# Adapter products of a unit's two halves from partitions 0 and 64, and the second gate's logits by experts in four quadrants

## The chip, the cores and the metric

The kernel runs on one core of one Trainium2 chip. The metric is the device time of one execution in microseconds; the time of a kernel is the median of its runs. Engines are named as in the profile: PE is TensorE, DVE VectorE, ACT ScalarE, POOL GpSimd, SP the queue that issues most DMAs.

## What is computed

The input x has 8 batches of 256 tokens of 128 features. Two layers follow each other, each added to its input, each with a conditioning step and a feed-forward over 8 experts of width 512. All is float32.

```python
# layer 0: masked pooling over the batch's tokens, then all 8 experts on every token, weighted by kept gate logits
pooled = softmax(mask(tanh(x @ W1 + b1) @ v)) @ x / count
logits = pooled @ gate_weight.T            # kept where >= the value at rank 4*128*6 of all, else 0
x = x + sum_e gates[..., e] * (gelu_tanh(pooled @ w1[e].T + b1[e]) @ w2[e].T + b2[e])
# layer 1: an adapter chosen by the batch's language, layer norm, then the 2 best of 8 experts per token
h = relu(x @ W1[lang] + b1[lang])          # 128 -> 32
a = layernorm(x + h @ W2[lang] + b2[lang]) * gamma[lang] + beta[lang]      # 32 -> 128
xn = layernorm(a) * gamma + beta
w = top-2 of softmax(xn @ gate_w), made to sum to 1
x = x + a + sum_e w_e * (gelu(xn @ w1[e] + b1[e]) @ w2[e] + b2[e])
```

## The kernel before

The 2048 tokens are 16 tiles of 128. They are handled in five units: units 0, 1 and 2 are four tiles each (two batches), units 3 and 4 are two tiles each (one batch). GT is 4, P is 128, D is 128, A is 32, E is 8.

**Layer 0.** The first hp_first starts at 36.1 us, after the pooling of the first batches. From there `layer` loops over units and, in each, over the 8 experts: four products hp_first (L801, up to 128x512), each with its GELU on ScalarE (L803), and, one expert behind, four accumulated products yp_first (L781). VectorE multiplies each yp_first by its gates, which SP loads spread over the partitions (gbc_first, L761), and adds it up in acc_first (L769, L771).

**What runs behind.** A queue of generators, `behind`, is worked off between those products: `pump()` takes one step of the first generator, up to its next `yield`, at each call. After a unit's last expert, `adapt(u)` is put into this queue, so units 0 to 3 are adapted behind the products of later units, and unit 4 behind layer 1. A scheduler then orders the instructions of every engine by its own estimate of when they can run; each engine's order is fixed when the kernel is built.

**`adapt(u)`** goes through these steps:
- x2T, the unit's x by features, is acc_first plus xT (L578). fp (L459) turns acc_first to tokens, and x2 (L582) is x by tokens.
- adp (L588): for each of the unit's batches one product of lw1 (128x32, the batch's language) with that batch's 256 columns of x2T. All outputs lie on partitions 0 to 31 of one PSUM bank, side by side. ha (L590) is the ReLU with the bias, one VectorE instruction per batch; its 33rd row is set to one by POOL (L586), which carries the bias of the next product.
- dp (L595): for each tile one product of 33 rows of ha with lw2 (33x128), all into one bank. xr (L598) adds x2 to it in one instruction.
- Two layer norms (`normed`: statistics on VectorE, the power rstd_l and rstd_f on POOL, L475), and the rows zr for the experts.
- znp (L624) turns the rows to features, znT (L629) scales them.
- l1p (L635): for each tile the logits of the second gate, with the tile's znT as stationary operand (128x128) and the 8 columns of the gate's weights streamed. lg (L638) copies them, `top_one` twice picks two experts per token.
- kp (L666, L667) counts, by products with ones and a triangle, how many earlier tokens went to each expert; from that pos (L686) is each token's row, and POOL scatters the rows to xs in DRAM, one indirect DMA a tile and choice (L688), eight in a unit of four tiles.
- For units 2, 3 and 4, lists of the expert tiles that are then full are made (`listed`).

**Layer 1.** 36 expert tiles of 128 rows. `fetch(k)` has SP load the rows xt (L831) and the first weights wt (L839) of the expert named in the list: tiles 0 to 16 come from unit 2's list, 17 to 20 from unit 3's, and from 21 on unit 4's. A load waits until the scatters that can fill it have landed. `turn` transposes (xtp, L846), `hidden` makes four products hps (L857) and the GELU hs (L859), `output` four products yps (L866), bias (L870), weight (L871) and an indirect DMA to ys (L872) from POOL. At the end ys is loaded again (yg, L890), added to the residual (L899, L900) and stored (L904).

**Buffers.** PSUM is cut into four banks "big" (psb: hp_first, adp, dp, znp, hps), two "y" (psy: yp_first, yps) and two "sm" (pss: fp, l1p, kp, xtp). ha has two buffers.

**Loads of the adapters.** Near the start SP reads each batch's language number and loads lw1, lw2 and the language's gamma and beta (lgb), three DMAs for each of 8 batches (L164).

Of the kernel before, what the change touches and what calls it, by code (L numbers as in the profile page):

```python
# [10 lines left out]
F32 = mybir.dt.float32  # L11
I32 = mybir.dt.int32
AF = mybir.ActivationFunctionType
ALU = mybir.AluOpType
AX = mybir.AxisListType
SYNC = mybir.DependencyInfo(mybir.DependencyClass.Sync, mybir.DependencyReason.DATA)
SP, PE, DVE = mybir.EngineType.SP, mybir.EngineType.PE, mybir.EngineType.DVE
# [4 lines left out]
B, S, D = 8, 256, 128  # L22
P = 128
NT = B * S // P
NG = 4
GT = NT // NG
GN = GT * P

UNITS = [(0, 0, 4), (1, 0, 4), (2, 0, 4), (3, 0, 2), (3, 2, 2)]
NU = len(UNITS)  # L30
SLOTS = {2: 17, 3: 21, 4: 39}
E, HC = 8, 4
A = 32
NL = 10
KTH = 4 * 128 * 6 - 1
NEG = -1.0e30
# [21 lines left out]
C_W1 = 0  # L58
C_G0 = C_W1 + A
C_G1 = C_G0 + E  # L60
# [5 lines left out]
C_LB = C_LG + 1  # L66
NCOL = C_LB + 1
XW = D + E + 1


@with_exitstack
def tile_adaln_ffn_d2(ctx: ExitStack, tc: tile.TileContext, x, ptype, lang, cols, b1v,
                      w10, w20, w11d, w21d, lw1, lw2, lgb, out):
    nc = tc.nc
# [3 lines left out]
    const = ctx.enter_context(tc.tile_pool(name="const", bufs=1))  # L78
    first = ctx.enter_context(tc.tile_pool(name="first", bufs=E))
    keep = ctx.enter_context(tc.tile_pool(name="keep", bufs=NG))  # L80
    work = ctx.enter_context(tc.tile_pool(name="work", bufs=2))
    small = ctx.enter_context(tc.tile_pool(name="small", bufs=4))
    dram = ctx.enter_context(tc.tile_pool(name="dram", bufs=1, space=DRAM))
    psb = ctx.enter_context(tc.tile_pool(name="psb", bufs=4, space=PSUM))
    psy = ctx.enter_context(tc.tile_pool(name="psy", bufs=2, space=PSUM))
    pss = ctx.enter_context(tc.tile_pool(name="pss", bufs=2, space=PSUM))
# [4 lines left out]
    for g in range(NG):  # L91

        xg.append(keep.tile([P, GT, XW], F32, tag="xg", name=f"xg{g}"))
    ptb = const.tile([P, B], I32, name="ptb")
    lgi = const.tile([P, B], I32, name="lgi")
    col = const.tile([P, NCOL], F32, name="col")
    bva = const.tile([A, 2], F32, name="bva")
    ident = const.tile([P, P], F32, name="ident")
# [10 lines left out]
    for e in range(E):  # L109
        t = first.tile([P, HC * P], F32, tag="w1", name=f"w10_{e}")  # L110
        nc.sync.dma_start(out=t, in_=w10[e])
        w10s.append(t)
        t = first.tile([P, HC, D], F32, tag="w2", name=f"w20_{e}")
# [4 lines left out]
    for g in range(NG):  # L118
        nc.gpsimd.memset(xg[g][:, :, XW - 1:], 1.0)
    ones = const.tile([P, P], F32, name="ones")  # L120
# [31 lines left out]
    nc.vector.tensor_scalar(out8[:, 2:3], out8[:, 2:3], -1.0, NEG, ALU.mult, ALU.add)  # L152


    lws, las, lgs = [], [], []
    for b in range(B):
        at = nc.values_load(lgi[0:1, b:b + 1], engines=(SP,), min_val=0, max_val=NL - 1,
                            skip_runtime_bounds_check_because="a language's number")
        for lst, name, src, rows, width in (
                (lws, "lw1", lw1[bass.ds(at * P, P), :], P, A),  # L160
                (las, "lw2", lw2[bass.ds(at * (A + 1), A + 1), :], A + 1, D + 1),
                (lgs, "lgb", lgb[bass.ds(at, 1), :].rearrange("o w -> (o w)").partition_broadcast(P), P, 2 * D)):
            t = const.tile([rows, width], F32, name=f"{name}_{b}")
            nc.sync.dma_start(out=t, in_=src)  # L164
            lst.append(t)

# [13 lines left out]
    front = work.tile([P, HC, GN], F32, tag="hT", name="front").rearrange("p c n -> p (c n)")  # L180
    at = front[:, :GN].rearrange("p (g t a) -> p g t a", g=NG, a=A)
    fwd, bwd, top = (front[:, GN + i * S:GN + (i + 1) * S] for i in range(3))
    fwd, bwd, rows = fwd[:B, :], bwd[:B, :], top[:B, :]
# [17 lines left out]
    def products(g):  # L201

        space = (psy, "y") if g < 2 else (psb, "big")
        xa = space[0].tile([P, GT, A + E], F32, tag=space[1], name=f"xa{g}")
        for t in range(GT):
# [18 lines left out]
    for g in range(NG):  # L224
# [8 lines left out]
        if not g:  # L233
            nc.tensor.matmul(bvp.rearrange("p c a -> p (c a)"), lhsT=ones[:A, :],
                             rhs=diag.rearrange("k c a -> k (c a)"), start=True, stop=True)
# [9 lines left out]
    for b in range(B):  # L245
        kinds.append(nc.values_load(kind[0:1, b:b + 1], engines=(DVE,), min_val=0, max_val=2,
                                    skip_runtime_bounds_check_because="2 - 2 e0 - e1, of flags"))
# [14 lines left out]
    for g in range(NG):  # L262
        tp = psb.tile([P, 2, S], F32, tag="big", name=f"top{g}")
        for i in range(2):
            nc.tensor.matmul(tp[:, i, :], lhsT=ident[:, 2 * g + i:2 * g + i + 1].to_broadcast([P, P]), rhs=top,
                             start=True, stop=True)
# [15 lines left out]
    def pool(b, space):  # L282
        m, g, i = masks[b], b // 2, b % 2
        pp = space[0].tile([P, 2, XW], F32, tag=space[1], name=f"poolp{b}")
        for jt in range(2):
# [104 lines left out]
    while known < half + 1:  # L390
        n = min(known, half + 1 - known)
# [126 lines left out]
    for e in range(E):  # L518
        nc.sync.dma_start(out=w21[:, e, :], in_=w21d[e].rearrange("p c d -> p (c d)"))
    nc.sync.dma_start(out=b2all.rearrange("p e d -> p (e d)"),  # L520
                      in_=b2d.rearrange("e d -> (e d)").partition_broadcast(P))
    rows = xs.rearrange("(p m t) c -> p m (t c)", p=P, t=GT)
# [11 lines left out]
    def tiles_of(counts, edges, name, f=None):  # L534

        c2 = small.tile([P, E, NT], F32, tag="c2", name=f"c2_{name}", bufs=1)
        nc.vector.tensor_tensor(c2, counts.unsqueeze(2).to_broadcast([P, E, NT]),
                                edges.unsqueeze(1).to_broadcast([P, E, NT]), ALU.is_ge)
        if f is None:
            f = small.tile([P, E], F32, tag="f", name=f"nf_{name}", bufs=2)  # L540
        nc.vector.tensor_reduce(f, c2, AX.X, ALU.add)
        return f
# [30 lines left out]
    def adapt(u, acc):  # L573
        g, o, nt = UNITS[u]
        n, t0 = nt * P, g * GT + o
        batches = range(t0 // 2, (t0 + nt) // 2)
        x2T = work.tile([P, GN], F32, tag="x2T", name=f"x2T{u}")[:, :n]
# [3 lines left out]
        x2 = work.tile([P, GT, D], F32, tag="x2", name=f"x2_{u}")[:, :nt, :]  # L581
        nc.vector.tensor_tensor(x2, fp, xg[g][:, o:o + nt, :D], ALU.add)  # L582
        yield
        hp = psb.tile([A, 2, S], F32, tag="big", name=f"adp{u}")
        ha = work.tile([A + 1, 2, S], F32, tag="ha", name=f"ha{u}")
        nc.gpsimd.memset(ha[A:A + 1, :, :], 1.0)  # L586
        for i, b in enumerate(batches):
            nc.tensor.matmul(hp[:, i, :], lhsT=lws[b], rhs=x2T[:, i * S:(i + 1) * S], start=True, stop=True)  # L588
        for i, b in enumerate(batches):
            nc.vector.tensor_scalar(ha[:A, i, :], hp[:, i, :], las[b][:A, D:D + 1], 0.0, ALU.add, ALU.max)  # L590
        yield
        yield
        dp = psb.tile([P, GT, D], F32, tag="big", name=f"dp{u}")[:, :nt, :]
        for t in range(nt):
            nc.tensor.matmul(dp[:, t, :], lhsT=ha[:, t // 2, (t % 2) * P:(t % 2 + 1) * P],  # L595
                             rhs=las[batches[t // 2]][:, :D], start=True, stop=True)
        z = work.tile([P, GT, D], F32, tag="xr", name=f"xr{u}")[:, :nt, :]
        nc.vector.tensor_tensor(z, dp, x2, ALU.add)  # L598
        yield
        yield from normed(z, z, f"l{u}")  # L600
        yield
# [23 lines left out]
        if nt == GT:  # L625
            zt = keep.tile([P, GN], F32, tag="poolT", name=f"znT{u}")
        else:
            zt = work.tile([P, n], F32, tag="znT", name=f"znT{u}", bufs=1)
# [1 line left out]
                                col[:, C_LB:C_LB + 1], ALU.mult, ALU.add)  # L630
        yield
        yield
        lp = pss.tile([P, GT, E], F32, tag="sm", name=f"l1p{u}")[:, :nt, :]
        for t in range(nt):
            nc.tensor.matmul(lp[:, t, :], lhsT=zt[:, t * P:(t + 1) * P], rhs=col[:, C_G1:C_G1 + E],  # L635
                             start=True, stop=True)
        lg = small.tile([P, GT, E], F32, tag="ex", name=f"lg{u}")[:, :nt, :]
        nc.vector.tensor_copy(lg, lp)  # L638
        oh1, l1 = top_one(lg, f"p{u}")
# [31 lines left out]
        at = small.tile([P, GT, E], F32, tag="at", name=f"at_{u}")[:, :nt, :]  # L671
# [9 lines left out]
        for s, oh in enumerate((oh1, oh2)):  # L681
# [5 lines left out]
            for t in range(nt):  # L687
                move = nc.gpsimd.indirect_dma_start(  # L688
                    out=xs, out_offset=bass.IndirectOffsetOnAxis(ap=pos[:, t:t + 1], axis=0),
                    in_=zr[s][:, t, :], in_offset=None)  # L690
# [8 lines left out]
        if u in SLOTS:  # L699

            k0, k1 = SLOTS.get(u - 1, 0), SLOTS[u]
            f = tiles_of(counts, begun if u == NU - 1 else full, str(u))
# [218 lines left out]
    def early():  # L921
        for k in range(LEAD + PRIMED):
            ahead(k)
        for _ in range(PRIMED):
            flipped.append(turn(*fetched.popleft()))

    behind.append(run("poolings", poolings()))
    behind.append(run("threshold", threshold()))
    layer("first", AF.Gelu_apprx_tanh, poolT, w10s, w20s, C_B10, C_B20, gates0, "pool", adapt,
          early)  # L930

# [16 lines left out]
    while behind:  # L948
# [3 lines left out]
                          skip_runtime_bounds_check_because="a count of tiles")  # L952
# [62 lines left out]
```

## Time and profile before

| | us |
|---|---|
| median of 3 runs | 379.78 |
| lowest and highest | 378.04, 383.52 |
| the profiled execution | 373.48 |
| its span, first to last instruction | 371.8 |

| engine | busy, us | share | instructions |
|---|---|---|---|
| PE | 349.5 | 94% | 1596 |
| PEld | 237.9 | 64% | 1596 |
| DVE | 198.9 | 53% | 835 |
| ACT | 166.6 | 45% | 387 |
| POOL | 95.5 | 26% | 141 |

PE is the matrix multiply and PEld the load of its stationary operand. A line of the timeline gives start, duration, engine, source line, operation, output<-inputs, shapes and a count, and in brackets how long the engine stood idle before it and what ended that. A line of a waits view gives engine, output and line that waited, what released it, and total us, times and longest. A line of the groups gives engine, operation and shape with the count, then busy us and mean ns of one, then idle before it. Durations of products overlap with those of their neighbours; the time from one group's start to the next group's start is what the group took from the engine.

### The profile page before, as it was taken

Reading aid. Unit: us, or ns where it says so; the run is one execution under the profiler, and the core shown is the slowest. Engines: PE = TensorE matmul, PEld = TensorE weight load, DVE = VectorE, ACT = ScalarE, POOL = GpSimd, SP = SyncE. Lnnn points to the kernel's source line nnn. Section 1 sums busy time; section 2 is a strip of 40 time slices with the busy share of each in tenths; the row PEclk is TensorE's granted clock in tenths of the full one; section 3 lists DMA queues with packets and bytes.
Section 4 is the critical chain, followed back from the end, with each engine's and each line's share of the span. In section 5 each row is a group of like instructions: output and inputs, shape, how many; then the busy total and the mean of one; then the engine's idle time right before and its main releaser. Section 6 shows DMA issues by size and latency. Waiting matters only on the chain. (4 is left out here: it accounts for less than half of the span.)

```text
span 371.8 us, 5944 instructions
## 1 busy us (share of the span) xinstructions
PE 349.5 (94%) x1596; PEld 237.9 (64%) x1596; DVE 198.9 (53%) x835; ACT 166.6 (45%) x387; POOL 95.5 (26%) x141
## 2 busy tenths in 40 slices
PE   6999999999999999999999999999999989989950
PEld 5979545444444444544544468887887989979940
DVE  3358465554314567556461146578658668433353
ACT  2116733454453324522335233643563675857650
POOL 8100000000000003055126001207304656744550
PEclk9999999999999999999999999999999999999995
DMA  6934899200523321111013000112474355576556
GB/s 187 389 89 135 301 382 379 88 0 2 160 71 81 91 56 31 56 60 54 31 36 89 16 28 21 45 36 80 129 178 145 113 168 154 164 192 203 151 172 198
DMA packets 34466, 46.12 MB, mean 124 GB/s; under 512 B 5444, under 2 KB 17622, under 8 KB 34432
## 3 DMA queue, kind: packets, MB, share of 16 engines
q1 hardware_dynamic: 29888, 39.98, 35.3%
q0 software_dynamic: 2304, 4.37, 3.4%
q10 hardware_dynamic: 2240, 1.38, 1.2%
q8 instruction: 14, 0.23, 0.3%
q14 instruction: 20, 0.16, 0.1%
HBM read 31.57 MB, written 14.39 MB: 124 GB/s over the span
## 5 line engine op out<-in xcount | busy, mean ns | idle before, releaser
L803 ACT ACTIVATE hT_first<-hp_first,col 128x512 f32<-128x512 f32 (+1 forms) x160 | 93.5, 601 | 101.2 <-PE hp_first L801 101.0
L801 PE MATMUL hp_first<-poolT,w 128*128 128x512 f32 (+1 forms) x320 | 120.6, 512 | 0.0
L781 PE MATMUL yp_first<-hT_first,w 128*128 128x512 f32 (+1 forms) x320 | 120.5, 511 | 0.0
L781 PEld LDWEIGHTS yp_first<-hT_first,w 128*128 128x128 f32 x320 | 58.9, 190 | 42.5 <-issue 38.3
L801 PEld LDWEIGHTS hp_first<-poolT,w 128*128 128x128 f32 x320 | 59.0, 190 | 42.2 <-issue 36.8
L688 POOL DMA_INDIRECT xs<-zr,pos x32 | 32.2, 1008 | 65.3 <-DVE pos L686 27.9
L859 ACT ACTIVATE hs<-hps,b 128x128 f32<-128x128 f32 x144 | 40.5, 373 | 9.5 <-PE hps L857 9.5
L872 POOL DMA_INDIRECT ys<-yt,xt x36 | 35.5, 987 | 32.9 <-ACT hs L859 21.1
L769 DVE SCALAR_TENSOR_TENSOR part_first<-yp_first,col,gbc_first 128x512 f32<-128x512 f32 (+1 forms) x28 | 17.2, 615 | 40.5 <-PE yp_first L781 40.3
L866 PE MATMUL yps<-w,hs 128*128 x288 | 38.0, 276 | 0.5 <-ACT hs L859 0.5
L857 PE MATMUL hps<-xc,wt 128*128 128x128 f32 x288 | 38.2, 276 | 0.0
L857 PEld LDWEIGHTS hps<-xc,wt 128*128 128x128 f32 x288 | 35.1, 192 | 0.6 <-issue 0.4
L866 PEld LDWEIGHTS yps<-w,hs 128*128 128x128 f32 x288 | 35.0, 192 | 0.6 <-ACT hs L859 0.6
L871 ACT ACTIVATE yt<-yt,xt 128x128 f32<-128x128 f32 x36 | 14.8, 413 | 18.3 <-ACT hs L859 7.3
L410 POOL DMA_DIRECT2D gd_L<-gT_L x1 | 0.7, 653 | 81.2 <-DVE gT_L L408 81.2
L771 DVE TENSOR_TENSOR acc_first<-acc_first,part_first 128x512 f32<-128x512 f32 (+1 forms) x35 | 20.1, 580 | 0.6
L586 POOL MEMSET ha<- 1x512 f32 x5 | 2.6, 516 | 67.6 <-PE dp L595 67.4
L850 DVE COPY b<-col 128x4 f32 x36 | 7.0, 196 | 20.8 <-ACT hs L859 18.1
L789 ACT ACTIVATE y_first<-yp_first,col 128x512 f32<-128x512 f32 x8 | 5.5, 687 | 24.2 <-PE yp_first L781 24.2
L848 DVE TENSOR_SCALAR xc<-xtp,col 128x128 f32<-128x128 f32 x36 | 14.4, 401 | 1.9 <-PE xtp L846 1.9
L870 DVE TENSOR_TENSOR yt<-yps,b2all 128x128 f32<-128x128 f32 x36 | 10.4, 290 | 9.1 <-PE yps L866 7.9
L424 DVE TENSOR_SCALAR_CACHE_REDUCE fl<-logit,tr 128x128 f32<-128x128 f32 x46 | 13.5, 343 | 0.6
(213 smaller groups left out, 327.9 us busy)
## 6 DMA issues: line engine op xcount, KB each, us to landing
wt<-in_w_dram SPq DMA_DIRECT2D x36, 256.0 KB
xs<-empty SPq DMA_DIRECT2D x1, 8580.0 KB
w<-in_w_dram SPq DMA_DIRECT2D x24, 256.0 KB
gbc_first<-gd_L SPq DMA_DIRECT2D x24, 256.0 KB
xt<-xs SPq DMA_DIRECT2D x36, 65.0 KB
gbc_first<-gd_L SPq DMA_DIRECT2D x16, 128.0 KB
yg<-ys SPq DMA_DIRECT2D x5, 256.0 KB
lgb<-in_lgb_dram SPq DMA_DIRECT2D x8, 128.0 KB
```

The costliest lines, as they stand in the source:

```text
L688: move = nc.gpsimd.indirect_dma_start(out=xs, out_offset=bass.IndirectOffsetOnAxis(ap=pos[:, t:t + 1], axis=0), in_=zr[s][:, t, :], in_off ...
L769: nc.vector.scalar_tensor_tensor(part, y, bias, gbc, ALU.add, ALU.mult)
L771: nc.vector.tensor_tensor(accs[u], accs[u], part, ALU.add)
L781: nc.tensor.matmul(yp, lhsT=w2s[e][:, c, :], rhs=hT[:, c, :], start=(c == 0), stop=(c == HC - 1))
L801: nc.tensor.matmul(hp, lhsT=w1s[e][:, c * P:(c + 1) * P], rhs=sources[g][:, o * P:o * P + n], start=True, stop=True)
L803: nc.scalar.activation(hT[:, c, :], hp, act, bias=col[:, cb1 + e * HC + c:cb1 + e * HC + c + 1])
L848: nc.vector.tensor_scalar(xc, tp, col[:, C_LG:C_LG + 1], col[:, C_LB:C_LB + 1], ALU.mult, ALU.add)
L857: nc.tensor.matmul(hp[:, c, :], lhsT=wt[:, c * P:(c + 1) * P], rhs=xc, start=True, stop=True)
L859: nc.scalar.activation(hT[:, c, :], hp[:, c, :], AF.Gelu, bias=b1[:, c:c + 1])
L866: nc.tensor.matmul(yp, lhsT=hT[:, c, :], rhs=w21[:, bass.ds(ek, 1), c * D:(c + 1) * D], start=(c == 0), stop=(c == HC - 1))
L871: nc.scalar.activation(yt, yt, AF.Copy, scale=xt[:, D + 1:D + 2])
L872: move = nc.gpsimd.indirect_dma_start(out=ys, out_offset=bass.IndirectOffsetOnAxis(ap=xt.bitcast(I32)[:, D:D + 1], axis=0), in_=yt, in_off ...
```

## The change

There are three edits, and the loads that go with them.

1. `halves(u)` gives the batches of a unit's two halves: two batches, or the same batch twice. For each half, adp's product writes its own partitions: 0 to 31 for the first, 64 to 95 for the second, in the same columns of the bank. In a unit of two tiles each half is 128 columns of the one batch, so there are two products of 128 columns where there was one of 256. ha has the two halves on partitions 0 to 32 and 64 to 96, with a row of ones at 32 and at 96.
2. dp's products of the first half read partitions 0 to 32, those of the second 64 to 96. They alternate, and each half has a PSUM tile of its own, two "big" banks where there was one. The sum xr is one instruction per half.
3. In units of four tiles the logits are made the other way round: 32 columns of `col` from the gate's 8 on are the stationary operand, and a tile's 128 columns of znT are streamed; tile t's result goes to partitions 32t to 32t + 31 of one bank (l1q). Of each 32 rows the first 8 are the logits. VectorE copies the bank (l1s), two `yield`s follow, one transpose on PE turns it to tokens (l1p), and lg reads 8 of every 32 columns. Units of two tiles are as before.
4. lw2 is loaded into one tile per unit, once for each half, so the two small units load theirs twice: ten loads of lw2 where there were eight. The language numbers are read ahead of the loads in the program.

```diff
+LANE = 64
...
+def halves(u):
+
+    g, o, nt = UNITS[u]
+    b = (g * GT + o) // 2
+    return (b, b + 1) if nt == GT else (b, b)
...
+    for u, (g, o, nt) in enumerate(UNITS):
+        la = const.tile([LANE + A + 1, D + 1], F32, name=f"lw2_{u}")
+        las.append(la)
+        for i, b in enumerate(halves(u)):
...
+            nc.sync.dma_start(out=la[i * LANE:i * LANE + A + 1, :], in_=lw2[bass.ds(langs[b] * (A + 1), A + 1), :])
...
-        hp = psb.tile([A, 2, S], F32, tag="big", name=f"adp{u}")
-        ha = work.tile([A + 1, 2, S], F32, tag="ha", name=f"ha{u}")
-        nc.gpsimd.memset(ha[A:A + 1, :, :], 1.0)
-        for i, b in enumerate(batches):
-            nc.tensor.matmul(hp[:, i, :], lhsT=lws[b], rhs=x2T[:, i * S:(i + 1) * S], start=True, stop=True)
-        for i, b in enumerate(batches):
-            nc.vector.tensor_scalar(ha[:A, i, :], hp[:, i, :], las[b][:A, D:D + 1], 0.0, ALU.add, ALU.max)
+        m, lanes = n // 2, [slice(0, A), slice(LANE, LANE + A)]
+        hp = psb.tile([LANE + A, S], F32, tag="big", name=f"adp{u}")[:, :m]
+        ha = work.tile([LANE + A + 1, S], F32, tag="ha", name=f"ha{u}")[:, :m]
+        for lane in lanes:
+            nc.gpsimd.memset(ha[lane.stop:lane.stop + 1, :], 1.0)
+        for i, b in enumerate(halves(u)):
+            nc.tensor.matmul(hp[lanes[i], :], lhsT=lws[b], rhs=x2T[:, i * m:(i + 1) * m], start=True, stop=True)
+        for lane in lanes:
+            nc.vector.tensor_scalar(ha[lane, :], hp[lane, :], las[u][lane, D:D + 1], 0.0, ALU.add, ALU.max)
...
-        dp = psb.tile([P, GT, D], F32, tag="big", name=f"dp{u}")[:, :nt, :]
-        for t in range(nt):
-            nc.tensor.matmul(dp[:, t, :], lhsT=ha[:, t // 2, (t % 2) * P:(t % 2 + 1) * P],
-                             rhs=las[batches[t // 2]][:, :D], start=True, stop=True)
+        dps = [psb.tile([P, 2, D], F32, tag="big", name=f"dp{u}_{i}") for i in range(2)]
+        for t in range(nt // 2):
+            for i, lane in enumerate(lanes):
+                rows = slice(lane.start, lane.stop + 1)
+                nc.tensor.matmul(dps[i][:, t, :], lhsT=ha[rows, t * P:(t + 1) * P], rhs=las[u][rows, :D],
+                                 start=True, stop=True)
...
-        nc.vector.tensor_tensor(z, dp, x2, ALU.add)
+        for i in range(2):
+            part = slice(i * nt // 2, (i + 1) * nt // 2)
+            nc.vector.tensor_tensor(z[:, part, :], dps[i][:, :nt // 2, :], x2[:, part, :], ALU.add)
...
+        if nt == GT:
+
+            lq = pss.tile([P, P], F32, tag="sm", name=f"l1q{u}")
+            for t in range(nt):
+                nc.tensor.matmul(lq[t * A:(t + 1) * A, :], lhsT=col[:, C_G1:C_G1 + A], rhs=zt[:, t * P:(t + 1) * P],
+                                 start=True, stop=True)
+            ls = work.tile([P, P], F32, tag="gT", name=f"l1s{u}")
+            nc.vector.tensor_copy(ls, lq)
+            yield
+            yield
+            lp = pss.tile([P, GT, A], F32, tag="sm", name=f"l1p{u}")
+            nc.tensor.transpose(lp.rearrange("p t c -> p (t c)"), ls, ident)
+            lp = lp[:, :, :E]
+        else:
...
```

In the order that the scheduler makes of the changed kernel, the transpose of the logits stands two hp_first products (units 0 and 1) or four (unit 2) behind l1q. Unit 4's kp stands three yps and three hps products further back on PE than before. On POOL its rstd_l stands one output scatter further ahead, and one more output scatter stands ahead of its four scatters to xs instead of between them.

More of the change, by code (lines that the diff above doesn't have):

```diff
@@ L155, in tile_adaln_ffn_d2 @@
     lws, las, lgs = [], [], []
[L156 to L165, printed above, removed]
+    langs = [nc.values_load(lgi[0:1, b:b + 1], engines=(SP,), min_val=0, max_val=NL - 1,
+                            skip_runtime_bounds_check_because="a language's number") for b in range(B)]
+    for u, (g, o, nt) in enumerate(UNITS):
+        la = const.tile([LANE + A + 1, D + 1], F32, name=f"lw2_{u}")
+        las.append(la)
+        for i, b in enumerate(halves(u)):
+            if nt == GT or not i:
+                t = const.tile([P, A], F32, name=f"lw1_{b}")
+                nc.sync.dma_start(out=t, in_=lw1[bass.ds(langs[b] * P, P), :])
+                lws.append(t)
+            nc.sync.dma_start(out=la[i * LANE:i * LANE + A + 1, :], in_=lw2[bass.ds(langs[b] * (A + 1), A + 1), :])
+            if nt == GT or not i:
+                t = const.tile([P, 2 * D], F32, name=f"lgb_{b}")
+                nc.sync.dma_start(out=t, in_=lgb[bass.ds(langs[b], 1), :].rearrange("o w -> (o w)").partition_broadcast(P))
+                lgs.append(t)
     logit = const.tile([P, E, NT], F32, name="logit")
@@ L632, in adapt @@
         yield
[L633 to L636, printed above, removed]
+        if nt == GT:
[11 more added lines that the diff above has]
+        else:
+            lp = pss.tile([P, GT, E], F32, tag="sm", name=f"l1p{u}")[:, :nt, :]
+            for t in range(nt):
+                nc.tensor.matmul(lp[:, t, :], lhsT=zt[:, t * P:(t + 1) * P], rhs=col[:, C_G1:C_G1 + E],
+                                 start=True, stop=True)
         lg = small.tile([P, GT, E], F32, tag="ex", name=f"lg{u}")[:, :nt, :]
```

## The prediction

> **What bounds the kernel now.** I read the page first, then the waits of TensorE, then the timeline of TensorE around the first unit's adapter, then the groups of the lines that change, and last the timelines where the last unit's rows reach the expert tiles.
>
> ```profile
> PE 349.5 (94%) x1596; PEld 237.9 (64%) x1596; DVE 198.9 (53%) x835; ACT 166.6 (45%) x387; POOL 95.5 (26%) x141
> ...
> PE   6999999999999999999999999999999989989950
> ```
>
> TensorE is busy 8 or 9 tenths in every slice from the second to the thirty-eighth. A busy row can hide waits, so the second view is its list of waits:
>
> ```profile
> PE idle L193 <- POOL ident masks.py:199: 2.6, 1, 2.6
> PE xtp L846 <- DMA xt<-xs: 1.7, 1, 1.7
> PE kp L666 <- DVE sofar L660: 1.2, 1, 1.2
> PE znp L624 <- DVE zr L478: 0.8, 1, 0.8
> ```
>
> After the start it waits some 4 us in all. TensorE's own work, in its order, is the bound, so time taken from its queue comes off the end, except where one of these waits takes it back. The third view gives what the touched lines cost, read from start to next start (the durations overlap and are too long for that):
>
> ```profile
> 132.73 1.05 PE L588 MATMUL adp<-x2T,lw 128*32 128x256 f32 x4
> 133.71 1.98 PE L781 MATMUL yp_first<-hT_first,w 128*128 128x512 f32 x4
> 135.62 1.16 PE L595 MATMUL dp<-lw,ha 33*128 33x128 f32 x8
> 136.71 1.98 PE L781 MATMUL yp_first<-hT_first,w 128*128 128x512 f32 x4
> 138.53 3.60 PE L801 MATMUL hp_first<-poolT,w 128*128 128x512 f32 x8
> 141.96 3.60 PE L781 MATMUL yp_first<-hT_first,w 128*128 128x512 f32 x8
> ...
> 153.56 0.95 PE L635 MATMUL l1p<-col,znT 128*128 128x8 f32 x8
> 154.37 2.82 PE L801 MATMUL hp_first<-poolT,w 128*128 128x512 f32 x6
> ```
>
> adp takes 133.71 - 132.73 = 0.98 us, dp 1.09, l1p 0.81. Units 1 and 2 give 0.98, 1.08 to 1.09 and 0.81 again; the units of two tiles give 0.55 for adp and 0.64 for dp. All the touched work is 3 x 2.88 + 2 x 1.19 = 11.0 us, 2.9% of the run: no speed-up of it can bring more than that.
>
> ```profile
> L595 PE MATMUL dp<-lw,ha 33*128 33x128 f32 x32 | 4.9, 288 | 0.0
> L588 PE MATMUL adp<-x2T,lw 128*32 128x256 f32 x16 | 4.4, 386 | 0.0
> L635 PEld LDWEIGHTS l1p<-col,znT 128*128 128x128 f32 x32 | 4.3, 191 | 1.1 <-DVE znT L629 0.5 <-issue 0.5
> ```
>
> The counts matter: 8 written adp products stand as 16 records and 16 dp products as 32. A written f32 product is two load-and-multiply pairs on the same part of the array, one after the other.
>
> **The skill.** The Trainium skill's "TensorEngine Tiling (Array Packing)", Key Properties, says that different tiles of the array load and multiply in parallel, and that changing the tiling mode drains TensorE. Its "TensorE: Matmul & The Clock Gate", Part 3 ("What overlaps and what doesn't"), says that multiplies start and end in program order, a second tile's some 4 ns after the first's, and gives 3.07x for four row tiles and 2.38x for three column tiles, at 512 columns. No run of before uses two tiles, so overlap isn't shown here. The drain fits: hp_first gives 3.43 / 8 = 0.429 us for 512 columns, so 0.214 for 256 and 0.107 for 128; adp's four passes then leave 0.98 - 0.86 = 0.12 us over and dp's eight 1.09 - 0.86 = 0.23. The tiling page's Gotcha 1 says that row tiles must write different PSUM banks; that is why dp becomes two tiles.
>
> **The change, part by part.** *adp.* The two halves go to columns 0 and 64. In program order the passes are a0 a1 b0 b1; a1 must follow a0 in its tile, b0 may run beside a1, b1 follows: three slots for four. A four-tile unit saves 0.21 us. A two-tile unit replaces two passes of 256 (0.43) by four of 128 in three slots (0.32): 0.11. Bounds: nothing (no overlap), or two slots (0.43 and 0.21 saved).
>
> *dp.* Lanes alternate, eight passes of 128: a0, a1 with b0, b1 with the next a0 and so on, five slots: 0.32 saved, and 0.11 in a two-tile unit. The weight loads are 128 wide and fill these slots too, so this needs loads of the two row halves to run side by side. Bounds: nothing saved, or 0.43.
>
> *Logits.* Today 0.81 us: eight loads of 128 columns, 0.10 each, for 8 streamed columns. New: four products with 32 weight columns streaming 128, eight passes. By the same rule five slots, 0.53, plus a switch of mode as adp's, 0.12, plus one transpose at 0.11 (znp: four in 151.84 - 151.40 = 0.44): 0.77, a saving of 0.05. Bounds: no overlap, 0.86 + 0.23 = 1.09, which loses 0.27; four quadrants together, two slots, 0.44, which saves 0.37. This part can lose; it is near even.
>
> Sum over TensorE: 3 x (0.21 + 0.32 + 0.05) + 2 x (0.11 + 0.11) = 1.74 + 0.44 = 2.2 us, 0.2 of it in unit 4.
>
> *New waits.* The transpose waits for VectorE's copy of 128x128 from PSUM (the row of gT_L has 0.29 us), in units 0 to 2. Behind the waiting transpose in TensorE's order stand all the expert products, for which ScalarE waits. The order that the scheduler gave puts two products of 512 columns (1.7 us) or four of 256 ahead of it, cover for one VectorE instruction in progress (at most 0.81 in its rows) and the copy. Without that cover it would be 1 us a unit; with it I take 0.1 each, 0.3 in all, bounds 0 to 2. The gate's chain of these units gets later by two pump steps; unit 2's rows are first loaded at 262.33 and first used at 278.76, so 16 us hide the 1 to 2 us.
>
> *VectorE.* Per four-tile unit one more copy (0.29) and the sum over dp in two of 256 columns (2 x 0.42 for 0.69); VectorE is at 53% and gets 0.45 us more: nothing. PSUM: dp holds two of the four "big" banks. The next product that needs either comes behind at least four other passes or after yps and hps; dp's sum starts within 1.2 us of it, so nothing, and up to 1 us if VectorE runs late.
>
> *SP and POOL.* Ten loads of lw2 where there were eight: two more on SP at some 0.45 us each (two lw loads take 0.87) between 15.5 and 32 us, in front of w21 and the fill of xs. The next thing in that queue that can be late is gbc_first at 94.57, which waits for gd_L anyway. The memset of ha becomes two rows of half the length; the queue behind it is held by the same dp as before. Nothing.
>
> *Unit 4's chain.* This is where the saving can be given back. Its rows are finished only during the expert tiles:
>
> ```profile
> 315.15 0.95 POOL L688 DMA_INDIRECT xs<-zr,pos  x1 [0.30 <-issue]
> ```
>
> ```profile
> 325.16 1.07 SPq L831 DMA_DIRECT2D xt<-xs  x1
> ...
> 327.73 0.30 PE L846 MATMUL xtp<-ident,xt 128*128 128x128 f32 x1 [1.71 <-DMA xt<-xs]
> ```
>
> From the end of the last acc_first (283.16) to this transpose run 44.6 us, a chain through VectorE, POOL and DMAs, and TensorE waits 1.71 us for it. What TensorE saves inside that stretch, 0.2 us, only lengthens the wait; what it saves before 283 moves the start of the chain and counts in full. What lengthens the chain counts in full too. ha becomes two instructions of 128 columns (0.33 each by the slope, for 0.47) and the sum two (0.29 each for 0.42): +0.35 us. Against it, POOL's rstd_l of unit 4 comes ahead of an output scatter that it stands behind today (its input is done at 290.71, it starts at 292.01): up to -1.3. Both end at kp, whose place in TensorE's order is now three yps and three hps products further back (six times 0.22 us, 1.3), while today it holds TensorE for 1.21 us: kp runs 0.1 us later than before, with its inputs ready. After kp, POOL sends one more output scatter ahead of unit 4's four instead of between them, so the last of the four keeps its place. I take 0.2, bounds -0.5 to 2.
>
> **Together.** -2.0 (before 283) + 0.3 + 0.2 = -1.5 us. The profiled execution took 373.48 (span 371.8 and 1.68 around it), so I expect 372.0 there. The median of the runs shown, 379.78, is 6.3 higher; nothing in the change touches that, so 378.3. A measurement of this kernel can tell about 2% from no change, 7.6 us; the forecast lies within.
>
> **The rivals.**
> *All passes overlap* (the upper bounds: 3 x 1.23 + 2 x 0.43 = 4.5, 4.1 of it before 283; with a chain unchanged and 0.1 for the waits): -4.0, 375.8. For it speak the skill's two factors; against it that a product's two passes share one tile and end in order.
> *Nothing overlaps*: adp and dp as before, logits 3 x 0.27 = +0.8, waits 0.3, chain 0.2: +1.3, 381.1. For it: l1p at 0.10 us for 8 columns shows that loads alone can be the bound, and dp's are as wide.
> *Slower by unit 4's chain*: its last scatter leaves POOL at 315.15, 32.0 us after the last acc_first. Each microsecond more goes to the end. From 33.7 us (the 1.7 that is saved) the kernel is slower than before; with two tiles' time (2 x 1.89 us, the step from one xtp to the next) it is 379.78 - 1.7 + 3.8 = 381.9. For it: the chain already makes TensorE wait, the scheduler moved kp back and an output scatter ahead. Against: POOL's last scatter keeps its place.
>
> **How the numbers follow.** Forecast 0.53, full overlap 0.22, no overlap 0.13, late chain 0.12. The runs shown spread over 378.04 to 383.52, 1.4%, so a case 4 us from the old median can come out past 2%. Faster by over 2%: half of full overlap and a little of the forecast, 0.17. Slower by over 2%: half of the late chain, and 0.04 of the others, 0.10. Within 2%: 0.73. The range goes from full overlap less the spread, 373.8, to the late chain with a little more, 383.0.
>
> **What would show it.** adp's block from 0.98 to about 0.77 us from start to next start, dp's from 1.09 to 0.77, l1q and the transpose together 0.7 to 0.8; records of one lane that start beside the other's. The last acc_first some 1.7 us earlier, and a wait of xtp for xt of 1.7 to 3 us. I am wrong if the blocks keep their length, if a transpose waits over 0.5 us for l1s, if hp_first waits for dp's banks, or if a wait over 4 us stands at xtp.

## The result, and the profile after

Median 377.50 us (372.88 to 384.24, 22 runs) against 379.94 us for the kernel before in the same measurement (376.03 to 385.04, 22 runs): ratio 0.9941, 95% interval 0.9914 to 0.9968. That is 2.2 us less by the ratio and 2.4 between the medians; 1.5 were forecast. The profiled execution took 377.19 us, span 375.4.

An execution starts in one of two ways, with the first hp_first at 29.0 to 31.4 us or at 36.1 to 36.4 us in the profiles here, and the kernel before shows both. Where two traces are compared below, times are therefore counted from that first hp_first. This execution ends 346.35 us after it, and the profiled one of before 335.66 us after its own, although the medians go the other way; the experiments on the third chip bear on that.

The page, first the busy times, then TensorE's busy tenths and its granted clock in 40 slices:

```profile
PE 344.7 (92%) x1603; PEld 230.1 (61%) x1603; DVE 200.3 (53%) x845; ACT 167.1 (45%) x387; POOL 96.1 (26%) x146
...
PE   6899999999999999999999999989979996999940
...
PEclk9999999999999999999999999999998998999995
```

TensorE is busy 4.8 us less than before, and still the engine without gaps until about the 27th slice. Then come holes that the profile of before did not have, and its list of waits shows two sorts of them:

```profile
PE xtp L882 <- DVE xc L884: 2.6, 2, 1.9
PE xtp L882 <- issue: 1.9, 2, 1.1
PE kp L702 <- DVE sofar L696: 1.8, 4, 0.8
PE yps L902 <- issue: 1.7, 2, 1.4
PE hp_first L837 <- issue: 1.1, 2, 0.6
```

The third line is a dependence: kp waited once before, in unit 4; now it waits four times. The lines that end in "issue" are time in which TensorE waits for nothing that the profile shows. The experiments separate the two.

TensorE's timeline around unit 0's adapter and second gate; blocks are read from start to next start, as for before:

```profile
125.67 0.62 PE L605 MATMUL adp<-x2T,lw 128*32 128x256 f32 x4
126.23 1.98 PE L817 MATMUL yp_first<-hT_first,w 128*128 128x512 f32 x4
128.14 0.71 PE L615 MATMUL dp<-lw,ha 33*128 33x128 f32 x8
128.79 1.98 PE L817 MATMUL yp_first<-hT_first,w 128*128 128x512 f32 x4
...
145.73 0.42 PE L659 MATMUL l1q<-znT,col 128*32 128x128 f32 x8
146.09 1.98 PE L837 MATMUL hp_first<-poolT,w 128*128 128x512 f32 x4
147.91 0.27 PE L666 MATMUL l1p<-ident,l1s 128*128 128x128 f32 x1
148.02 1.02 PE L837 MATMUL hp_first<-poolT,w 128*128 128x512 f32 x2
```

adp went from 0.98 to 0.56 us, dp from 1.09 to 0.65, the logits from 0.81 to 0.36 + 0.11 = 0.47. These are the prediction's upper bounds, 0.43 and 0.43 saved, and 0.34 of 0.37. The groups of the same lines:

```profile
L615 PE MATMUL dp<-lw,ha 33*128 33x128 f32 x32 | 3.4, 325 | 0.0
L605 PE MATMUL adp<-x2T,lw 128*32 128x256 f32 x12 | 1.9, 391 | 0.0
L659 PE MATMUL l1q<-znT,col 128*32 128x128 f32 x24 | 1.3, 285 | 0.0
```

The sums fall because records now lie on each other, not because one is shorter: a dp record is 325 ns long where it was 288. The mean of a group does not show an overlap; the starts do.

The end of unit 4's chain in this execution (its last scatter, and the transposes of the first three tiles that hold its rows):

```profile
312.24 0.96 POOL L724 DMA_INDIRECT xs<-zr,pos  x1 [0.30 <-issue]
...
327.22 0.38 PE L882 MATMUL xtp<-ident,xt 128*128 128x128 f32 x2
329.12 0.33 PE L882 MATMUL xtp<-ident,xt 128*128 128x128 f32 x1 [0.62 <-DVE xc L884]
```

Before, the third of these transposes waited 1.71 us for xt; here it waits 0.62 us.

### The profile page after: what moved, and what is told of

Same layout as the page of the kernel before. It is cut to its first block, busy times and chain, and to the rows that moved or that the text cites. A ratio compares the mean times of both kernels' runs of the same rounds, so it can differ in the third digit from the quotient of the medians.

```text
span 375.4 us, 5988 instructions
## 1 busy us (share of the span) xinstructions
PE 344.7 (92%) x1603; PEld 230.1 (61%) x1603; DVE 200.3 (53%) x845; ACT 167.1 (45%) x387; POOL 96.1 (26%) x146
## 3 DMA queue, kind: packets, MB, share of 16 engines
q0 software_dynamic: 2304, 4.37, 3.4%
## 5 line engine op out<-in xcount | busy, mean ns | idle before, releaser
L817 PE MATMUL yp_first<-hT_first,w 128*128 128x512 f32 (+1 forms) x320 | 122.3, 518 | 0.0
L817 PEld LDWEIGHTS yp_first<-hT_first,w 128*128 128x128 f32 x320 | 59.7, 194 | 42.9 <-issue 38.6
L902 PE MATMUL yps<-w,hs 128*128 x288 | 39.6, 281 | 3.1 <-issue 1.7
L893 PE MATMUL hps<-xc,wt 128*128 128x128 f32 x288 | 39.9, 283 | 0.0
L902 PEld LDWEIGHTS yps<-w,hs 128*128 128x128 f32 x288 | 36.1, 196 | 2.6 <-issue 1.8
L893 PEld LDWEIGHTS hps<-xc,wt 128*128 128x128 f32 x288 | 36.7, 199 | 1.1 <-DMA wt<-in_w_dram 0.6
L603 POOL MEMSET ha<- 1x256 f32 (+1 forms) x10 | 2.6, 262 | 63.7 <-PE dp L615 63.2
L882 PE MATMUL xtp<-ident,xt 128*128 128x128 f32 x36 | 10.0, 287 | 4.7 <-DVE xc L884 2.6
```

The lines of the kernel that those rows point to most:

```text
L817: nc.tensor.matmul(yp, lhsT=w2s[e][:, c, :], rhs=hT[:, c, :], start=(c == 0), stop=(c == HC - 1))
L893: nc.tensor.matmul(hp[:, c, :], lhsT=wt[:, c * P:(c + 1) * P], rhs=xc, start=True, stop=True)
L902: nc.tensor.matmul(yp, lhsT=hT[:, c, :], rhs=w21[:, bass.ds(ek, 1), c * D:(c + 1) * D], start=(c == 0), stop=(c == HC - 1))
```

## The experiments

Three questions were open after this profile. Do all passes of the pairs overlap, as the blocks say, so that a part of the gain is given back somewhere, and by which part of the change? Does the order of the lanes matter, as the forecast's rule had it? (A lane is one half's part of the array: the rows from 0 or from 64 for dp, the columns from 0 or from 64 for adp.) And are the holes marked "issue" made by the paired products?

### The four on a first chip

e1 is the changed kernel, e4 the kernel before. e2 takes the adapters' part alone, e3 the logits' part alone:

```diff
 # e2: the changed kernel, but
-        if nt == GT:
-            lq = pss.tile([P, P], F32, tag="sm", name=f"l1q{u}")
...
-        else:
-            lp = pss.tile([P, GT, E], F32, tag="sm", name=f"l1p{u}")[:, :nt, :]
...
+        lp = pss.tile([P, GT, E], F32, tag="sm", name=f"l1p{u}")[:, :nt, :]
 # e3: the kernel before, with these lines the other way round
```

> The changed kernel once more. In the profile after, TensorE stood still after unit 3's dp (0.57, 0.52 and 0.72 us between 252 and 255) and before two yps and an xtp near 315 us (0.32, 1.37, 1.14), and VectorE and ScalarE were released in steps of 1.42 us there. If the overlapped pairs delay TensorE's signals, the steps stand at unit 3's dp again, in the same place. If they are a disturbance of that one execution, they are gone or elsewhere. Either way the blocks are adp 0.56, dp 0.65, l1q 0.36 us from start to next start. Time: ratio to before 0.994, 0.990 to 0.998.

> adp and dp in two lanes, the logits as before. If what TensorE saves comes off the end wherever nothing takes it back, this keeps 3 x 0.86 + 0.42 = 3.0 us of the 4.0 us saved ahead of the last acc_first, and none of the waits of kp in units 0 and 1 (0.44 us each in the profile after): about -2.5 us, ratio 0.993. If the logits brought the gain, it is 0.998 or more.

> The logits by experts alone, the adapters as before. l1q and the transpose take 0.47 us for 0.81, so 1.0 us is saved in three units; the longer chain (copy, transpose, two steps) lets kp wait for sofar in units 0 and 1, as after (0.44 us each). If these waits come from the logits, they stand here again and the sum is -0.2 us, ratio 0.999 to 1.000. If they don't, the ratio is 0.997.

> The kernel before once more, one look. If the stretches of slow release come from the overlapped pairs, none is seen here: TensorE has only waits for sofar at unit 4's kp and for xt at unit 4's first tile, as in its first profile. If they are a disturbance of executions of either kernel, they can stand here too. The waits by cause (kp, znp, xtp) repeat within 0.5 us otherwise.

Ratios: changed kernel 0.9924 (0.9871 to 0.9977), adapters alone 0.9985 (0.9906 to 1.0064), logits alone 1.0011 (0.9978 to 1.0043). The intervals are too wide to tell the parts from each other, so the traces are read here. TensorE's time from the first hp_first to the end of the last, each record from its start to the next one's, by tile (us; not all tiles are listed):

| | before (e4) | changed (e1) | adapters (e2) | logits (e3) |
|---|---|---|---|---|
| adp + dp | 7.38 | 4.37 | 4.37 | 7.38 |
| l1q + l1p | 2.79 | 1.75 | 2.79 | 1.76 |
| idle before kp | 0.00 | 1.06 | 0.00 | 1.06 |
| idle before znp | 0.14 | 0.42 | 0.50 | 0.42 |
| kp | 1.18 | 1.32 | 1.18 | 1.31 |
| yp_first | 108.32 | 109.35 | 108.48 | 109.35 |
| all, the rest too | 240.69 | 238.82 | 238.23 | 241.85 |

The blocks save 3.01 + 1.04 = 4.05 us: full overlap, where the forecast's rule gives 2.0. What comes back is 2.18 us, and the columns say from which part: the adapters alone return 0.55 of their 3.01 (mostly znp's wait), while the logits alone save 1.03 in their blocks and cost 2.19 elsewhere, +1.16 in all. The last acc_first ends 247.06 us after the first hp_first in the kernel before, 245.11 in the changed one, 244.60 with the adapters alone, 248.04 with the logits alone.

Why the logits cost: TensorE's timeline at unit 0's kp, in the kernel before (e4) and in the changed one (e1).

```profile
150.21 1.88 PE L781 MATMUL yp_first<-hT_first,w 128*128 128x512 f32 x4
151.93 0.31 PE L666 MATMUL kp<-sofar,ones 128*128 128x40 f32 x2
```

```profile
151.21 2.74 PE L817 MATMUL yp_first<-hT_first,w 128*128 128x512 f32 x6
154.39 0.39 PE L702 MATMUL kp<-sofar,ones 128*128 128x40 f32 x2 [0.44 <-DVE sofar L696]
```

In the kernel before, the six hp_first and four yp_first records between the logits and kp cover VectorE's chain from lg to sofar. Here the copy and the transpose start that chain later, the transpose and kp have only 2 + 6 records between them, and TensorE waits 0.44 us. The wait costs more than the bracket says: from 151.21 to 154.39 are 3.18 us, and six records at 0.429 us from start to start are 2.57, so 0.61 us are lost for a bracket of 0.44. The missing 0.16 us stand in the last yp_first. A record of this form is 0.592 us long, wait or not, and in an unbroken row the next one starts after 0.429; here no product lies on the last 0.163 us. Units 0 to 2 wait so, which makes about half of yp_first's extra 1.03 us.

The paired products alone don't make the holes: e1 issues every pair of the changed kernel, and after its first hp_first no wait of TensorE over 0.15 us is marked "issue", as two at 252.1 and 253.4 us were in the first profile.

Behind the last acc_first the parts differ too. The adapters alone end 330.80 us after the first hp_first, the kernel before 335.29 and the changed one 333.51: of the 4.49 us that the adapters alone gain in these traces, 2.03 come in the expert tiles, where unit 4's chain runs. No run takes that stretch apart.

### Order of the lanes, and dp eight times over, on a second chip

```diff
 # e5: the changed kernel, but
-        for t in range(nt // 2):
-            for i, lane in enumerate(lanes):
+        for i, lane in enumerate(lanes):
+            for t in range(nt // 2):
 # e6: the kernel before, but
-        for t in range(nt):
+        for t in [*range(nt)] * 8:
 # e7: the changed kernel, but
-        for t in range(nt // 2):
+        for t in [*range(nt // 2)] * 8:
```

> The changed kernel with the two loops of dp's products exchanged: first all products of one lane, then all of the other, so that neighbours in the order share their rows of the array. Theory A (two products run side by side only where they stand next to each other in the order and have different rows): in a four-tile unit only the pair in the middle overlaps, dp's block from start to next start is 0.85 to 1.0 us instead of 0.65, in a two-tile unit (one product a lane, same order as before) it stays at 0.42. Theory B (the order doesn't matter, each lane has its own queue): 0.65 again. Theory C (the gain of dp comes from its smaller tiles of PSUM or its two sums): 0.65 again. In the time, A costs 3 x 0.3 = 0.9 us, too little to see in one run; the blocks decide.

One run, 383.05 us, which says nothing of half a microsecond; its timeline does:

```profile
135.17 0.72 PE L615 MATMUL dp<-lw,ha 33*128 33x128 f32 x8
135.82 1.55 PE L817 MATMUL yp_first<-hT_first,w 128*128 128x512 f32 x3
```

0.65 us again, and the point after the second unit's gate (the 193rd hp_first record) at 176.75 us against 176.72 in e1: e5's theory A falls. If every product had to start behind all those ahead of it, lane one's first pass would follow lane zero's four, at least 0.3 us later; in the records the passes start in pairs, 13 ns apart. So lanes run beside each other though the order has them one after the other. B and C stay; e6 and e7 test C.

> The kernel before with each of dp's products issued eight times over into the same place. The block of a four-tile unit was 1.09 us, 0.86 of it passes: it should grow by 7 x 0.86 = 6.0 us to about 7.1, that of a two-tile unit by 7 x 0.43 = 3.0 us to 3.65. All units: 3 x 6.0 + 2 x 3.0 = 24 us more than the kernel before, where TensorE's order sets the end and for unit 4 where its chain does.

> The changed kernel with each of dp's products issued eight times over, in alternating lanes. Theory A (two lanes side by side, both passes of each): the passes of a four-tile unit take 0.43 us, so 7 x 0.43 = 3.0 us more, a block of 3.65, and 1.5 us more in a two-tile unit, a block of 1.9; 12 us more than the changed kernel in all, and 12 to 14 us less than the kernel before with eight. Theory B (the forecast's rule, a lane's second pass beside the other lane's first, five slots of eight; in a long row of products it is one slot of two plus one, so this rule tends to the same half): the same 3.65 here; this run settles only that the overlap lasts. Theory C (no overlap; the shorter block comes from elsewhere): 7.1 us and the same time as the kernel before with eight.

420.95 us (ratio 1.1116, 1.1014 to 1.1218) and 401.26 us. The windows of the three four-tile dp blocks, first with the kernel before's products and then in lanes (columns: stretch, length, busy time of PE, PEld, DVE, ACT and POOL, granted clock, DMA share, GB/s):

```profile
128.80:139.70 10.90, 10.90 (x65) 10.68 (x64) 0.00 (x0) 0.00 (x0) 0.00 (x0) 0.66 0.01 2
171.40:180.60 9.20, 9.20 (x65) 9.04 (x64) 0.00 (x0) 0.00 (x0) 2.81 (x3) 0.78 0.09 31
238.98:247.60 8.62, 8.62 (x65) 8.42 (x64) 0.00 (x0) 0.58 (x2) 0.00 (x0) 0.84 0.06 17
```

```profile
129.20:133.00 3.80, 3.80 (x66) 3.67 (x65) 0.00 (x0) 0.00 (x0) 0.00 (x0) 1.00 0.02 4
164.90:170.40 5.50, 4.42 (x66) 4.05 (x65) 0.00 (x0) 0.00 (x0) 2.30 (x3) 1.00 0.12 39
227.30:231.10 3.80, 3.80 (x65) 3.65 (x64) 0.00 (x0) 0.62 (x2) 0.00 (x0) 1.00 0.14 39
```

Length times clock gives 7.2 us in each of the first three, for 7.1 expected: 64 passes one after the other, and the clock was cut besides. In lanes the same 64 passes take 3.8 us at full clock (the middle block has a hole of about 1.1 us without a wait), for 3.65 expected. Theory C falls: the gain is the overlap and not the new tiles or sums. e7's A and B both expected 3.65; between them the block of 0.65 us in the first profile and in e5 has decided for A. The 19.7 us between the medians are more than the 12 to 14 expected. At full clock e6's three blocks would take 21.6 us for the 28.7 shown, so an estimate of 7 us goes to the cut clock.

### One more step ahead of kp, and all four together on a third chip

```diff
 # e8 and e12: the changed kernel, but
-        yield
-        yield
+        for _ in range(3 if nt == GT else 2):
+            yield
         kp = pss.tile([P, GT + 1, E], F32, tag="sm", name=f"kp{u}")[:, :nt + 1, :]
```

> The changed kernel with one more step of the unit's chain between the sum sofar and kp in the four-tile units, which puts kp one product of 512 columns (0.86 us) further back in TensorE's order, two of 256 in the third unit. Theory A (kp waits 0.44, 0.44 and 0.18 us for sofar because the copy and the transpose made the gate's chain longer than the products ahead of kp cover): these waits go, and with each about 0.16 us in which TensorE runs empty ahead of it; the last acc_first ends some 1.3 to 1.6 us earlier after the first hp_first than in the changed kernel (247.06 us in the kernel before, 245.1 in the changed one), at about 243.7. The waits of znp, 0.42, may move. Theory B (the time lost around the logits is the change of tiling mode and the transpose's place, not kp's wait): the waits go and the last acc_first stays within 0.3 us of 245.1, because another instruction waits in kp's place (fp for acc_first, or znp). At the end unit 4's chain takes a part of it back: 0 to 1.5 us there.

374.22 us, ratio 0.9852 (0.9802 to 0.9902), on the second chip. e9 is the kernel before, e10 the changed kernel, e11 the adapters alone, e12 the extra step once more:

> The kernel before against itself, on the chip of the three runs beside it: a control. Ratio 1.000, its interval the width that the others' ratios have to be read against. Theory A (the stalls of TensorE after 250 us, without a wait and in steps of about 1.4 us, that several profiles on one chip show, come from the chip): if that chip does it here, this profile shows them too, and the granted clocks of the three others are like this one's. Theory B (they come from the denser work of the changed kernels): this profile has none and clocks of 0.984 and more, the three others have clocks of 0.96 to 0.98 in some executions.

> The changed kernel, beside the two below. Last acc_first 245.1 us after the first hp_first in an execution without stalls, kp's waits 0.44, 0.44 and 0.18 again; ratio 0.990 to 0.995 as in the two measurements so far (0.9941 and 0.9924).

> The part of adp and dp alone, with the second gate's logits as in the kernel before. Theory A (the logits' part costs time as it stands): last acc_first at 244.6, the end 2 to 3 us ahead of the changed kernel's when both are counted from the first hp_first, ratio 0.986 to 0.990. Theory B (the two parts are equal within the measurement, as the first ratios of 0.9985 and 0.9924 left open): ratio 0.990 to 0.998.

> The changed kernel with one more step ahead of kp in the four-tile units, once more, in an execution that may be without stalls. Theory A (kp's waits were what the logits' part gave away): last acc_first at about 243.7, 1.4 us ahead of the changed kernel; ratio 0.983 to 0.988, ahead of the changed kernel's by 0.3 to 0.8%. Theory B (the first ratio, 0.985, was luck of that chip): ratio within 0.2% of the changed kernel's.

| | median, us | ratio | 95% interval | 2nd gate done | last acc_first | end |
|---|---|---|---|---|---|---|
| before (e9) | 379.11 | 0.9990 | 0.9946 to 1.0033 | 177.69 | 247.09 | 345.40 |
| changed (e10) | 377.38 | 0.9934 | 0.9901 to 0.9968 | 176.75 | 248.49 | 343.55 |
| adapters (e11) | 372.85 | 0.9829 | 0.9776 to 0.9882 | 175.96 | 244.62 | 340.15 |
| extra step (e12) | 372.57 | 0.9806 | 0.9733 to 0.9879 | 175.40 | 248.58 | 341.06 |

(The last three columns are us after the first hp_first in the profiled execution; "2nd gate done" is the 193rd hp_first record.) The repetition of traces is close: e4 and e9 agree within 0.01 us at the second gate and 0.03 at the last acc_first.

The extra step does what theory A said, up to the second gate, where e8 and e12 agree on 175.40: 1.35 us less than the changed kernel in two units, that is 0.68 a unit: the wait of 0.45, the 0.16 behind the last record, and 0.07 of kp itself. Unit 0's kp in e12:

```profile
156.24 3.60 PE L817 MATMUL yp_first<-hT_first,w 128*128 128x512 f32 x8
159.67 0.31 PE L702 MATMUL kp<-sofar,ones 128*128 128x40 f32 x2
```

Eight records, 3.43 us, and no wait. Between the transpose and kp, unit 0 has ten records for eight now and unit 1 twelve for eight. In unit 2, against the expectation, the extra step left kp where it was in TensorE's order, 20 records behind the transpose, and its wait of 0.17 us stands in e8 and e12 too. Against the adapters alone e12 is 0.56 us ahead at the second gate: with cover, the logits' part pays 0.28 us a unit, of the 0.35 that its blocks save. At the last acc_first theory A's 243.7 was not reached (249.61 in e8, 248.58 in e12), since stalls without a wait stand in between, about 258 to 261 us in e12 and 249 to 255 in e10. So the waits of kp are shown as a cause up to the second gate; how much of the lower median is theirs, no run shows. The same six microseconds in e10, and then in e9 (columns as above):

```profile
249.00:255.00 6.00, 4.42 (x19) 3.02 (x20) 1.49 (x10) 1.57 (x5) 3.07 (x4) 1.00 0.22 65
```

```profile
249.00:255.00 6.00, 6.00 (x30) 4.98 (x29) 3.42 (x22) 1.81 (x4) 4.58 (x5) 1.00 0.24 80
```

In e10 TensorE is busy for 4.42 of the 6 us, at full clock, and VectorE for 1.49 where it was 3.42. These stalls come while unit 2's last scatters go out or just after: in e10 the first ends at 249.32 us, and the last scatter starts at 252.03. All five profiles with lanes and logits together on the second and third chip (e5, e7, e8, e10, e12) have them, and the first profile after; e6, e9 and e11, without the logits' part, don't, and no kernel on the first chip does. So neither of e9's theories holds as put: in these traces the stalls come only on such a chip and only with lanes and logits together. The logits alone were not run on such a chip, and what ties the stalls to them isn't settled. Later stalls of TensorE, some 245 to 249 us after the first hp_first, come to every kernel on the third chip: counted from the first hp_first, the end lies 10.1 us later there than on the first chip for the kernel before, 10.0 for the changed one, 9.4 for the adapters alone. The two first profiles differ like that, 335.66 and 346.35, so their last thirds should not be compared.

Much of the early stall is absorbed: e12 is 3.96 us behind e11 at the last acc_first and only 0.91 at the end. e11 bears its theory A out and goes beyond it: 244.62 at the last acc_first for 244.6, and an end 3.40 us ahead of the changed kernel's for 2 to 3, with the changed kernel's stalls in that difference. The two best versions can't be told apart by their ratios, and both are ahead of the changed kernel's 0.9934. The adapters alone are the simpler one.

## Why the prediction was right, and where its terms were not

The sum came out by luck in part: two errors of opposite sign cancel in it. Up to the last hp_first the blocks saved 4.05 us where 2.0 were forecast, and 2.18 came back where 0.3 were.

- *The bound.* TensorE's own order, with all touched work 11.0 us: held. Up to the last acc_first, in executions without stalls, 1.95 us were gained where 2.0 - 0.3 = 1.7 was forecast.
- *Three slots for four, five for eight.* This is the first step that failed. adp has two slots and dp four: 0.42 and 0.44 us saved instead of 0.21 and 0.32. The Trainium skill's "TensorEngine Tiling (Array Packing)", Key Properties, says that different tiles load and multiply in parallel, and that fits. The forecast then added from "TensorE: Matmul & The Clock Gate", Part 3 ("What overlaps and what doesn't"), that multiplies start in program order, and made a lane's second pass block the other lane's first. e5 contradicts that for dp: with the lanes one after the other in the order, the block is 0.65 us all the same. e6 and e7 show 7.2 against 3.8 us for 64 passes.
- *Logits near even.* Wrong in the same way: 0.81 went to 0.47 and not 0.77. The four column quadrants have their eight passes, 0.86 us one after the other, in a block of 0.36. No run changes the logits' order, so for them and for adp the overlap is read from the blocks.
- *The mode switch.* 0.12 and 0.23 us over the passes were assumed to stay. dp leaves 0.65 - 0.43 = 0.22 over, adp 0.56 - 0.43 = 0.13: they stayed.
- *New waits, 0.3 us.* The second failing term. The transpose did have its cover and does not wait for l1s, as argued. But the wait that counts is one further on, kp's for sofar, in units 0 to 2: 1.06 us shown; with the uncovered ends of records, znp's wait and the rest 2.18 came back in all. That kp's wait follows from the longer chain is shown by e3, which has it without the adapters' part, and by e8 and e12, where it goes in units 0 and 1. The text priced the new instruction's own wait, and let the later chain be hidden by the 16 us of unit 2's rows. It forgot that kp, in the middle of that chain, also stands in TensorE's order.
- *dp's two banks.* On the first chip no hp_first waits for them; nothing, as forecast. In four of the profiles with stalls one hp_first of unit 3's time does wait for xr, the sum that frees them: 0.7 us in the first profile after, e5 and e10, and 1.6 in e12. It is within the forecast's "up to 1 us if VectorE runs late" in three of four: in e10 dp's records end at 249.9 us and the first sum starts only at 253.05. That the two banks add to the stalls isn't excluded for the kernels with both parts; e11 has the same banks and no such wait.
- *Unit 4's chain, +0.2.* On the first chip the gain is 1.95 us at the last acc_first, 1.65 at unit 4's kp, 3.08 at its last scatter, and 1.78 at the end, so +0.17 in all. The size fits, the account behind it does not. The forecast said that the last scatter keeps its place; it came 1.4 us nearer to kp. A wait of xtp for xt of 1.7 to 3 us was to be seen; it is 0.62 us at unit 4's third tile in the first profile after and in e1, and e1 has one of 0.88 at a later tile. The 1.71 us of before were not the chain's length either: the transpose at 327.73 waits for the load issued at 323.34, not for the one at 325.16 shown beside it, and of that load all recorded parts but one had landed by 325.64, the last at 327.59. In e4 the wait is 0.77 us, at the second tile, and again for one late part (316.45, then 318.92).
- *Full overlap, the first rival.* Its mechanism is what happened; its time, 375.8, was missed because it kept 0.1 us for the waits. *Nothing overlaps* is excluded by the blocks. *Late chain*: not seen; the longest wait of xtp in the first profile after is 1.9 us, at 280 us, long before unit 4's rows.

## What to carry to other kernels

In this kernel small products on different row halves, column halves or column quadrants overlapped in full even in two-pass f32, less 0.13 to 0.22 us a block that stays; for dp the order of the lanes didn't matter. Read it from starts to next starts, since record means don't show it. Before pricing an inserted copy or transpose by its own wait, follow the chain to the next instruction that stands in the busy engine's order, and give that one cover too: here one and two products of 512 columns more ended the wait in two units; in the third the extra `yield` didn't move kp, and the wait stayed. Take an edit of two parts apart: here the adapters earned it and the logits ate a part of it, until one `yield` more made them pay up to the second gate.

## What had not been expected of the hardware

- 64 dp passes at one place of the array ran at a granted clock of 0.66 to 0.84, the same 64 in two lanes at 1.00 (e6, e7, one profile each). Which difference between the two blocks the clock answers to, their length or the single place, isn't shown.
- A wait of 0.44 us on TensorE cost 0.61 us: the record ahead of it is 0.592 us long where a next product starts after 0.429, and that end isn't counted as idle time.
- The longest waits for unit 4's rows in the kernel before came from one late part of a load, 2.0 and 2.5 us behind the others (327.59 after 325.64 us in its first profile, 318.92 after 316.45 in e4).
- On two of the three chips the engines stall in all kernels, near or after groups of indirect scatters, mostly without a wait that the profile shows (for instance hp_first at 253.40 and 254.81 us in e10, 1.41 us apart). Where those 10 us of the third chip come from, no run here shows.
